# Reordering the start, the weight fetch and the seams of a two-layer attention kernel

## The chip, the cores and the metric

The kernel runs on one core of one Trainium2 chip. The metric is the device time of one execution in microseconds; the median of three runs is compared. The kernel before takes 3128.49 us (3128.35 to 3129.97).

## The reference, cut to what matters

The input x has two images of 256 channels on 64 x 64 places. Two layers run, each on a group-normalised x, each added to x.

```python
# layer 0: attention over all 4096 places, 8 heads of 32 channels
qkv = einsum('bchw,oc->bohw', gn(x), qkv_w) + qkv_b
out = softmax(q^T k / sqrt(32)) v            # per head, 4096 x 4096
x = x + out
# layer 1: two block attentions (64 places each) and a 3x3 convolution
q, k, v = 1x1 convolutions of gn(x); positions are added to q and k
ctx   = block attention over places of one phase, 1x1, bn_relu   -> feats
ctx2  = block attention inside 8x8 blocks (two 1x1 with bn_relu each for q and k), 1x1, bn_relu
f_all = fc_w mixes heads of q, k, v;  out_conv = 3x3 convolution of f_all
x = x + rate1 * ctx2 + rate2 * out_conv
```

## The kernel before, in words

The channels lie on 128 partitions in KC = 2 halves, the 4096 places in NT = 8 tiles of T = 512. The outer loop runs over the two images b; for each there are four stages, each with its own pools of PSUM banks.

**Start and projections** (b = 0). `load_x` (L66) loads eight tiles of x, 512 KB each, with one SyncE DMA per tile (L70). `group_stats` (L331) takes two bn_stats per tile on VectorE (L308), joins them (L312), averages over groups of eight channels by a small matmul (L315, L325), and `normalise` writes xn (L350). `fold_scores` (L186) prepares layer 1's score matrix from weights alone: the weights `w_by_out`, which eight DMAs on ScalarE's queue load at the head of the program (L85, 64 partitions each), `place_rows` and `grid` (L90, L92, SyncE). It transposes (L194), multiplies (L206: pt_meet and the two pt_g; L215: pt_key), copies out of PSUM on ScalarE (L195 to L224), and stores the result `kept_g` (L225). In the kernel before it stands ahead of the statistics in the program. `project0` (L392) computes keys and queries of four heads at a time (L400, evicted at L405 on ScalarE and L406 on VectorE, stored at L409), then values (L423), then the other four heads. Tiles for stores come from the pool w4, which has twelve buffers. The GpSimd queue loads the small constants and the projection weights (L104, L115, L126, L130), each an own DMA. The tile framework gives every DMA one of eight completion semaphores per kind of queue, in turn; a DMA whose semaphore is still in use by an earlier one waits for that one to land, and SyncE issues in order.

**Attention of layer 0.** `attention0` holds an order written out by hand for TensorE, ScalarE and VectorE. Scores go to three PSUM tiles of 3, 2 and 2 banks (sa, sb, sc, L498), ScalarE takes the exponential (L504), TensorE multiplies with the values (`quarters`, L514), and VectorE (L551) or accumulating DMAs (L561) add the rows of exponentials for the denominators. One step is a group g (half a head's queries) and a block j of 128 keys, NJ = 32 blocks. For the last group the sums of the last three blocks go through matmuls with ones (`sum_rows`, L575). `steps` (L714) issues them at block NJ - 2, ahead of that block's and the last block's av matmuls, into a bank of the tag sb. `finish_last` (L611) then copies the sums (L624), takes the reciprocal (L625), copies av (L627), multiplies, adds x and feeds the statistics of layer 1.

**First half of layer 1.** `layer1_first` (L1073) again writes out the order for TensorE, ScalarE and VectorE: it regroups x (`to_groups`, L1084 on ScalarE, L1087 on VectorE and GpSimd), finishes the statistics of the second channel half (`st.means`, `st.spread`, `st.variances`), and, for b = 0, multiplies weights together in between. That is the generator `fold_products`: each `next(fold)` runs it to its next yield; the five pieces are transposes of w3 (L245), its product (L251), transposes of fv, its product, and the small product pb_lr (L260 to L266). Then eight tiles of block attention follow, written to feats (L1068). From its end on VectorE also makes the 3x3 weights for b = 0 (`conv_weights`, L823 to L871), stored to `wf_kept` in DRAM (L865).

**Second half of layer 1.** `layer1_second` (L1209) writes the normalised image xp (`to_image`, L1218 to L1221, all on ScalarE), runs the second block attention for eight tiles (L1269, L1278, L993, L1011, L1057), and between them sixteen steps of the 3x3 convolution in a transformed form: GpSimd transforms the image (`conv_transform`, L916, L920), TensorE multiplies (L930), VectorE transforms back (L936 to L957). `fetch_conv_weights` (L877) loads all of the weights, 4 MB, with one SyncE DMA (L880); for b = 0 it also transposes them, 64 matmuls (L889), evicted by VectorE and ScalarE in turn (L892, L894), and stores them back (L895). TensorE's order is written out there; ScalarE's, VectorE's and GpSimd's are set by the framework's scheduler.

Of the kernel before, what the change touches and what calls it, by code (L numbers as in the profile page):

```python
# [9 lines left out]
F32 = mybir.dt.float32  # L10
I32 = mybir.dt.int32
F32R = mybir.dt.float32r
AF = mybir.ActivationFunctionType
# [4 lines left out]
P = 128  # L18
B, C, H, W = 2, 256, 64, 64
# [21 lines left out]
def direct_layers(ctx: ExitStack, tc: tile.TileContext, a: dict, out: bass.AP, bad: bass.AP):  # L41
# [24 lines left out]
    def load_x(b):  # L66
        tiles = []
        for t in range(NT):
            xt = xpool.tile([P, KC, T], F32, tag="x", name=f"x_{b}_{t}")
            nc.sync.dma_start(  # L70
                out=xt,
                in_=a["x"][b, :, t * T : (t + 1) * T].rearrange("(k p) n -> p k n", p=P),
            )
            tiles.append(xt)
        return tiles

    by_out = {}
    for name in ("w1", "w2"):  # L80
        by_out[name] = wpool.tile([P, KC, C], F32, tag="wp", name=f"{name}_by_out")

        for i in range(4):
            r = 64 * (i % 2)
            nc.scalar.dma_start(  # L85
                out=by_out[name][r : r + 64, i // 2, :],
                in_=a["wx"][int(name == "w2"), :, i, 0:P:4, :],
            )
# [3 lines left out]
    nc.sync.dma_start(out=grid, in_=a["loc"][1:3, 0:64])  # L92
    meet = const.tile([2, P], F32, name="meet")
    nc.vector.memset(meet, 0.0)
    x_first = load_x(0)

    ident = const.tile([P, P], F32, name="ident")
    make_identity(nc, ident)
# [250 lines left out]
    def normalise(dst, src, k, mean, rstd):  # L349
        return nc.vector.tensor_scalar(dst, src, mean[:, k : k + 1], rstd[:, k : k + 1], ALU.subtract, ALU.mult)  # L350
# [106 lines left out]
    def attention0(b, xts, held):  # L457
# [105 lines left out]
        def work_of(g, j):  # L563


            if (g, j) < (last, NJ - 2):
                add_rows(g, j)
            for part in (None,) if j in (0, NJ - 1) else range(2):
                if part == 1:
                    yield  # L570
                quarters(
                    sums[g], held["v"][:, (g // 2) % 2, j, :], lambda u: unit(g, j, u), j == 0, j == NJ - 1, part
                )
# [140 lines left out]
        def steps():  # L714

            for done in range(NH0 * 2 * NJ):
                g, j = divmod(done, NJ)
                if (g, j) == (last, NJ - 2):
                    assert len(places) == n_units
                    held["rows"] = psum["sc"].tile([P, 2, T], F32, tag="sb", name=f"rows_{b}")[:, 1, :]  # L720
                    for i in (NJ - 2, NJ - 1):
                        add_rows(g, i)
                    sum_rows(g, held["rows"])
                for _ in work_of(g, j):
                    yield done
                if g and j == 0:

                    for w in range(2):
                        dst = added[g - 1][w]
                        for s in range(2) if w == 0 else (slice(0, 2),):  # L730
                            nc.vector.tensor_add(dst[:, s, :], dst[:, s, :], acc[s] if w == 0 else pair)
                    waiting.clear()
                if g and j == 1:
                    wanted.append(late[0].send)
                if g and j in (9, 17):
                    next(late[0])
                for what in also.get((g, j), ()):
                    what()
                if j == 4 and g % 2 == 0 and g // 2 + 1 < NH0:
                    fetch_head(b, g // 2 + 1, held)  # L740
                if j == NJ - 1:
                    waiting.append(g)
                    avs = w4([P, 2, T], f"avs_{b}_{g}")
                    if g < last:
                        nc.scalar.copy(avs[:, 0, :], sums[g])
                    copied[g] = avs
                    late[:] = [finish(g)]
                    next(late[0])
                    if g + 2 < NH0 * 2:
                        fetch_queries(b, g + 2, held)  # L750
                yield done + 1
# [125 lines left out]
    def fetch_conv_weights(b):  # L877

        wf = vpool.tile([P, KC, UW, C], F32, tag="vw", name=f"wf_{b}")
        nc.sync.dma_start(out=wf, in_=wf_kept)  # L880
        if b > 0:
            return wf
        for pos in range(UW):
            r, q = divmod(pos, 4)
            pw = bank([P, KC, C], f"pw_{pos}")
            for k in range(KC):
                for m in range(2):
                    block = slice(m * P, (m + 1) * P)
                    nc.tensor.transpose(pw[:, k, block], wf[:, k, pos, block], ident)  # L889
            scale = (0.5 if r in (1, 2) else 1.0) * (0.5 if q in (1, 2) else 1.0)  # L890
            if pos % 2:
                nc.scalar.activation(wf[:, :, pos, :], pw, AF.Copy, scale=scale)  # L892
            else:
                nc.vector.tensor_scalar(wf[:, :, pos, :], pw, scale, None, ALU.mult)  # L894
        nc.sync.dma_start(out=wf_kept, in_=wf)  # L895
        return wf
# [176 lines left out]
    def layer1_first(b, xts, put, check, st):  # L1073
# [64 lines left out]
        with tc.manual_schedule(engines={E.PE, E.Activation, E.DVE}):  # L1138
            st.aggregate(second)
            fold = fold_products() if b == 0 else iter(())  # L1140
            put(nc.gpsimd.tensor_copy, (0, 1))
            for t in range(5, NT):
                to_groups(0, t, nc.gpsimd)
            pm, pv = bank([P, 1], f"pm_l1_{b}"), bank([P, 1], f"pv_l1_{b}")
            for t in range(3):
                to_groups(0, t, nc.scalar)
                next(fold, None)
            to_groups(0, 3, nc.scalar)
            if b:
                to_groups(0, 4, nc.scalar)  # L1150
            st.means(second, pm, nc.vector.tensor_copy)
            st.spread(second)
            firsts = [lambda t=t, m=m: project(t, m, slice(0, 1)) for t in range(2) for m in range(KC)]
            if b:
                firsts.pop(0)()
            next(fold, None)
            st.variances(second, pv)
            st.deviations(second, pv)
            shift_of(st, 1)
            if b == 0:  # L1160
                to_groups(0, 4, nc.scalar)
            put(nc.gpsimd.tensor_copy, (2, 3))
            n_act = 2 + b
            for t in range(NT):
                done = to_groups(1, t, nc.scalar if t < n_act else nc.vector)
            for _ in fold:
                pass
            check()
            for first in firsts:
                first()  # L1170
            for t in range(2):
                for m in range(KC):
                    project(t, m, slice(1, KC))
            at_grid(0)
# [34 lines left out]
    def layer1_second(b, xts, feats, mean, rstd, shift, pacc, following):  # L1209
# [5 lines left out]
            nc.gpsimd.memset(xp[:, k, PADW - 1, :], 0.0)  # L1215
            nc.gpsimd.memset(xp[:, k, 1 : PADW - 1, 0 : PADW : PADW - 1], 0.0)

        def to_image(t):  # L1218
            for k in range(KC):
                nc.scalar.activation(  # L1220
                    xp[:, k, 1 + 8 * t : 9 + 8 * t, 1 : 1 + W], xts[t][:, k, :].rearrange("p (r w) -> p r w", w=W),  # L1221
                    AF.Identity, bias=shift[:, k : k + 1], scale=rstd[:, k : k + 1],
                )

        results = {}
        turns = [divmod(n, 4) for n in range(4 * NT // 2)]
# [26 lines left out]

        if b:
            for t in range(3):
                to_image(t)
            ahead[0] = conv_transform(b, xp, *turns[0])
        pending = None
        for t in range(NT):
# [87 lines left out]
    for b in range(B):  # L1347
        xts = x_first if b == 0 else ahead["xts"]
        w0 = w0_first if b == 0 else ahead["w0"]
        with tc.tile_pool(name=f"ps0_{b}", bufs=8, space=PSUM) as psum["ps"]:  # L1350
            if b == 0:
                fold_scores()
            mean, rstd = group_stats(xts, "l0_0") if b == 0 else ahead["stats"]
            xn = apool.tile([P, KC, N], F32, tag="A", name=f"xn_{b}")
            for t in range(NT):
                for k in range(KC):
                    normalise(xn[:, k, t * T : (t + 1) * T], xts[t][:, k, :], k, mean, rstd)
            held = project0(b, xn, w0)
        if b == 0:
            load_layer1()  # L1360
        load_set(b, ("w3",) if b == 0 else ("g", "w3"))
        with tc.tile_pool(name=f"sc_{b}", bufs=1, space=PSUM) as psum["sc"]:
            put, check, st = attention0(b, xts, held)
        with tc.tile_pool(name=f"ps1_{b}", bufs=8, space=PSUM) as psum["ps"]:
            between = layer1_first(b, xts, put, check, st)
        with (
            tc.tile_pool(name=f"pacc_{b}", bufs=1, space=PSUM) as pacc,
            tc.tile_pool(name=f"ps2_{b}", bufs=4, space=PSUM) as psum["ps"],
        ):
            layer1_second(b, xts, *between, pacc, following)  # L1370
# [558 lines left out]
```

## Time and profile before

| | us |
|---|---|
| median of three runs | 3128.49 (3128.35 to 3129.97) |
| profiled execution | 3126.4 |
| its span, first to last instruction | 3124.2 |
| TensorE (PE) busy | 3030.2 |
| VectorE (DVE) busy | 2457.5 |
| ScalarE (ACT) busy | 2315.7 |
| GpSimd (POOL) busy | 843.4 |
| statistics of x wait for its loads, in total | 21.3 |
| first projection matmul starts | 37.18 |
| TensorE stands still before the transposes of the 3x3 weights | 10.18 |
| TensorE stands still before the mean of image 1's second statistics | 6.76 |

How to read it: PE is TensorE's matmuls, PEld its weight loads, which overlap them, SP is SyncE, whose queue issues most DMAs; a name with q is an engine's sequencer. A timeline line gives start, duration, engine, line, operation, output<-input, their shapes, the number of instructions merged, and in brackets the idle time before with what ended it. A line of waits gives the waiter, the releaser, total time, times and the longest wait. A line of windows gives a stretch, its length, each engine's busy time and instructions, TensorE's granted clock (1.00 is full), the mean busy share of the 16 DMA engines, and GB/s.

### The profile page before, as it was taken

The numbers are of one execution on the slowest core, as the hardware profiler recorded it, in microseconds if no ns is written. First come the engines' busy times: TensorE is split into PE (matmuls) and PEld (weight loads), VectorE is DVE, ScalarE is ACT, GpSimd is POOL, SyncE is SP. The second block draws the span as 40 slices with busy tenths as digits, with TensorE's granted clock in tenths as the row PEclk, the third lists the DMA queues.
The fourth block names the chain that finished last, engine by engine and source line by source line (L and its number), as shares of the span: only waits on it lengthen the run. The fifth ranks groups of instructions, "written<-read, shape, count | busy, mean of one in ns | idle before, by whom it ended". The sixth has DMA issues, their size and how long they took to land. (4 is left out here: it accounts for less than half of the span.)

```text
span 3124.2 us, 62490 instructions
## 1 busy us (share of the span) xinstructions
PE 3030.2 (97%) x25049; PEld 1826.3 (58%) x25049; DVE 2457.5 (79%) x3121; ACT 2315.7 (74%) x2440; POOL 843.4 (27%) x939
## 2 busy tenths in 40 slices
PE   6999999999999999989999999999999999899998
PEld 3555555555555556667765555555555555466765
DVE  4589988989899999846545999989999999834543
ACT  2599999999999984622236999999999999834333
POOL 3022222222223221055400222222222222305440
PEclk9999999999999999999999999999999999999999
DMA  7979678797887761221159686897878975700000
GB/s 231 260 145 184 136 157 168 154 183 143 171 175 157 146 133 35 75 110 54 38 185 259 134 176 145 163 172 147 169 164 166 180 159 117 179 4 4 21 14 22
DMA packets 241623, 424.37 MB, mean 136 GB/s; under 512 B 98744, under 2 KB 109548, under 8 KB 238892
## 3 DMA queue, kind: packets, MB, share of 16 engines
q0 software_dynamic: 95504, 238.36, 39.7%
q1 hardware_dynamic: 145292, 181.41, 21.6%
q8 instruction: 198, 3.24, 0.4%
q14 instruction: 101, 0.83, 0.1%
q10 hardware_dynamic: 528, 0.52, 0.1%
HBM read 119.03 MB, written 68.39 MB: 60 GB/s over the span
## 5 line engine op out<-in xcount | busy, mean ns | idle before, releaser
L551 DVE TENSOR_TENSOR e<-e,es 128x1024 f32<-128x1024 f32 (+1 forms) x956 | 1039.5, 1147 | 77.6 <-ACT es L504 76.3
L514 PE MATMUL av<-es,v 128*32 128x256 f32 (+1 forms) x9644 | 746.4, 390 | 0.0
L551 DVE TENSOR_TENSOR e<-e,v 128x1024 f32<-128x1024 f32 (+1 forms) x640 | 676.2, 1113 | 50.9 <-ACT v L504 49.7
L504 ACT ACTIVATE es<-sa 128x1536 f32<-128x1536 f32 (+1 forms) x444 | 635.9, 1432 | 94.4 <-PE sa L498 55.4
L498 PE MATMUL sa<-q,k 128*128 128x512 f32 x1736 | 560.7, 430 | 9.2 <-ACT avs L588 3.5
L514 PE MATMUL av<-v 128*32 128x256 f32 (+1 forms) x6228 | 506.5, 389 | 0.0
L514 PEld LDWEIGHTS av<-es,v 128*32 128x32 f32 x9644 | 316.0, 109 | 299.5 <-issue 161.0
L498 PEld LDWEIGHTS sa<-q,k 128*128 128x128 f32 x1736 | 279.9, 188 | 292.2 <-issue 135.0
L498 PE MATMUL sc<-q,k 128*128 128x512 f32 x1180 | 371.5, 396 | 3.3 <-ACT v L504 1.3
L498 PE MATMUL sb<-q,k 128*128 128x512 f32 x1180 | 370.7, 395 | 1.3 <-ACT v L504 1.3
L514 PEld LDWEIGHTS av<-v 128*32 128x32 f32 x6228 | 216.5, 109 | 178.5 <-issue 81.2
L504 ACT ACTIVATE es<-sc 128x1024 f32<-128x1024 f32 x296 | 307.2, 1038 | 0.0
L504 ACT ACTIVATE v<-sc 128x1024 f32<-128x1024 f32 x294 | 305.0, 1038 | 1.7 <-DMA acc<-v 1.7
L504 ACT ACTIVATE es<-sb 128x1024 f32<-128x1024 f32 x296 | 302.3, 1021 | 1.4 <-DMA acc<-es 1.2
L504 ACT ACTIVATE v<-sb 128x1024 f32<-128x1024 f32 x294 | 300.2, 1021 | 2.7 <-DMA acc<-v 2.7
L498 PEld LDWEIGHTS sc<-q,k 128*128 128x128 f32 x1180 | 209.8, 187 | 75.9 <-ACT es L504 12.3
L498 PEld LDWEIGHTS sb<-q,k 128*128 128x128 f32 x1180 | 220.8, 188 | 56.1 <-ACT v L504 2.2
L504 ACT ACTIVATE v<-sa 128x1536 f32<-128x1536 f32 (+1 forms) x146 | 209.3, 1433 | 34.8 <-PE sa L498 15.1
L930 PE MATMUL mm<-v,wf 128*128 128x256 f32 x1024 | 230.3, 383 | 4.3 <-DVE z L939 4.3
L561 POOL DMA_DIRECT2D es<-es x116 | 99.0, 853 | 465.7 <-ACT es L504 394.4
L930 PEld LDWEIGHTS mm<-v,wf 128*128 128x128 f32 x1024 | 195.2, 192 | 40.4 <-issue 12.6
L920 POOL TENSOR_TENSOR v<-col 128x512 f32<-128x512 f32 x128 | 165.0, 1314 | 195.2 <-DVE x L951 44.7
(261 smaller groups left out, 3171.9 us busy)
## 6 DMA issues: line engine op xcount, KB each, us to landing
acc<-es POOLq DMA_DIRECT2D x128, 512.0 KB, 6.4
acc<-v POOLq DMA_DIRECT2D x84, 512.0 KB, 6.4
es<-es POOLq DMA_DIRECT2D x136, 256.0 KB, 4.4
v<-es POOLq DMA_DIRECT2D x132, 256.0 KB, 5.0
k<-wk_halves SPq DMA_DIRECT2D x64, 512.0 KB
q<-wq_halves SPq DMA_DIRECT2D x256, 128.0 KB
v<-v POOLq DMA_DIRECT2D x90, 256.0 KB, 5.1
es<-v POOLq DMA_DIRECT2D x86, 256.0 KB, 4.1
```

What stands on the lines that cost most here:

```text
L498: nc.tensor.matmul(sc[:, i, :], held["k", g // 2][:, j * P : (j + 1) * P], held["q", g, u // 2][:, u % 2, :], start=True, stop=True,)
L504: nc.scalar.activation(dst, sc[:, i : i + m, :], AF.Exp, scale=SC0)
L514: nc.tensor.matmul(dst[HD0 * u : HD0 * u + HD0, n], lhs, rhs(u)[:, n], start=start, stop=stop)
L551: nc.vector.tensor_add(dst[:, s, :], dst[:, s, :], src)
L561: nc.gpsimd.dma_start(out=dst, in_=src, accum_op=ALU.add)
L920: (nc.gpsimd.tensor_add if plus else nc.gpsimd.tensor_sub)(dst, rows(one), rows(two))
L930: nc.tensor.matmul(mm[:, m, r, :], wf[:, k, 4 * r + q, m * P : (m + 1) * P], v[r // 2][:, r % 2, k, :], start=k == 0, stop=k == KC - 1,)
```

## The change

It has five parts.

1. x is loaded at the head of the program. The eight loads of `w_by_out` move from ScalarE's queue to SyncE's, behind x, and `fold_scores` is called behind `project0` instead of ahead of the statistics.
2. The 3x3 weights are fetched by four DMAs of four positions each (1 MB, runs of 4 KB) instead of one.
3. The row sums of the last group are issued at block NJ - 3, one block sooner, into a bank of the tag sa.
4. In `layer1_first` one more piece of `fold_products` runs ahead of the mean matmul.
5. In `layer1_second`, for b = 1, the first three tiles of the second channel half of xp are written by VectorE instead of ScalarE.

```diff
+    x_first = load_x(0)
...
-            nc.scalar.dma_start(
+            nc.sync.dma_start(
                 out=by_out[name][r : r + 64, i // 2, :],
...
-    x_first = load_x(0)
...
-            if (g, j) < (last, NJ - 2):
+            if (g, j) < (last, NJ - 3):
                 add_rows(g, j)
...
-                if (g, j) == (last, NJ - 2):
+                if (g, j) == (last, NJ - 3):
                     assert len(places) == n_units
-                    held["rows"] = psum["sc"].tile([P, 2, T], F32, tag="sb", name=f"rows_{b}")[:, 1, :]
-                    for i in (NJ - 2, NJ - 1):
+                    held["rows"] = psum["sc"].tile([P, 3, T], F32, tag="sa", name=f"rows_{b}")[:, 2, :]
+                    for i in (NJ - 3, NJ - 2, NJ - 1):
                         add_rows(g, i)
                     sum_rows(g, held["rows"])
...
-        nc.sync.dma_start(out=wf, in_=wf_kept)
+        for r in range(4):
+            nc.sync.dma_start(out=wf[:, :, 4 * r : 4 * r + 4, :], in_=wf_kept[:, :, 4 * r : 4 * r + 4, :])
...
             if b:
                 to_groups(0, 4, nc.scalar)
+            next(fold, None)
             st.means(second, pm, nc.vector.tensor_copy)
...
-        def to_image(t):
+        def to_image(t, both=False):
             for k in range(KC):
-                nc.scalar.activation(
-                    xp[:, k, 1 + 8 * t : 9 + 8 * t, 1 : 1 + W], xts[t][:, k, :].rearrange("p (r w) -> p r w", w=W),
-                    AF.Identity, bias=shift[:, k : k + 1], scale=rstd[:, k : k + 1],
-                )
+                dst = xp[:, k, 1 + 8 * t : 9 + 8 * t, 1 : 1 + W]
+                src = xts[t][:, k, :].rearrange("p (r w) -> p r w", w=W)
+                if both and k == 1:
+                    normalise(dst, src, k, mean, rstd)
+                else:
+                    nc.scalar.activation(
+                        dst, src, AF.Identity, bias=shift[:, k : k + 1], scale=rstd[:, k : k + 1]
+                    )
...
             for t in range(3):
-                to_image(t)
+                to_image(t, True)
...
-            if b == 0:
-                fold_scores()
             mean, rstd = group_stats(xts, "l0_0") if b == 0 else ahead["stats"]
...
             held = project0(b, xn, w0)
+            if b == 0:
+                fold_scores()
```

## The prediction

> **What bounds the kernel now.** I read the page's shares and slices first, then, gap by gap, the waits and the timeline where TensorE (PE) stands still.
>
> ```profile
> PE 3030.2 (97%) x25049; PEld 1826.3 (58%) x25049; DVE 2457.5 (79%) x3121; ACT 2315.7 (74%) x2440; POOL 843.4 (27%) x939
> ...
> PE   6999999999999999989999999999999999899998
> ```
>
> PE is busy 97% of 3124.2 us, so no edit can save more than the 94 us it stands still and what it runs at reduced clock. The first slice is the worst. There the statistics wait for x (VectorE's, DVE's, timeline), and the x loads wait on their own queue (the waits of SyncE, SP):
>
> ```profile
> SPq L70 <- DMA w_by_out<-in_wx_dram: 11.1, 4, 8.4
> ...
> 31.32 1.29 DVE L308 BATCH_NORM_STATS2 stats_l<-x 128x6 f32<-128x512 f32 x2 [0.33 <-DMA x<-in_x_dram]
> ...
> 37.18 15.62 PE L400 MATMUL p_wk<-xn,wqk 128*128 128x512 f32 x32 [1.13 <-DVE xn L350]
> ```
>
> Four x loads waited 11.1 us for completions of the weight loads of L85, so the last of eight tiles reaches DVE at 31.32 and the first projection starts at 37.18. The table by windows shows why those weights are slow (the last columns are PE's granted clock, DMA share, GB/s):
>
> ```profile
> 8.00:12.00 4.00, 0.00 (x0) 0.00 (x0) 1.29 (x2) 0.95 (x1) 3.45 (x8) 1.00 0.16 49
> 12.00:26.00 14.00, 2.15 (x8) 1.14 (x8) 2.57 (x4) 1.68 (x11) 10.18 (x19) 1.00 1.02 281
> 26.00:31.00 5.00, 2.91 (x11) 2.76 (x12) 3.86 (x6) 0.18 (x1) 4.65 (x20) 1.00 0.18 57
> ```
>
> A share of 0.16 is about two of sixteen DMA engines. From 37.18 to 121.63 PE has no gap; then it turns to attention:
>
> ```profile
> 123.19 0.97 PE L498 MATMUL sa<-q,k 128*128 128x512 f32 x3 [1.56 <-DVE hl_wq L406]
> ...
> 123.21 1.28 ACT L504 ACT_TABLE_LOAD   x1 [0.86 <-DVE hl_wq L406]
> ...
> 124.51 1.45 ACT L504 ACTIVATE es<-sa 128x1536 f32<-128x1536 f32 x1
> ```
>
> The next large gap is the fetch of the 3x3 weights (timeline, then windows):
>
> ```profile
> 1328.70 0.33 SPq L880 DMA_DIRECT2D wf<-wf_kept  x1
> ...
> 1341.27 8.68 PE L889 MATMUL pw<-ident,wf 128*128 128x128 f32 x64 [10.18 <-DMA wf<-wf_kept]
> ...
> 1331.10:1341.20 10.10, 0.00 (x0) 0.00 (x0) 0.00 (x0) 0.78 (x1) 9.87 (x8) 0.65 0.84 363
> 1341.27:1344.40 3.13, 3.13 (x15) 3.13 (x16) 0.99 (x2) 0.60 (x1) 3.05 (x3) 0.50 0.01 3
> 1344.40:1347.50 3.10, 3.10 (x31) 3.10 (x30) 2.35 (x4) 1.93 (x4) 0.35 (x1) 1.00 0.00 0
> ```
>
> PE waits 10.18 us for 4 MB and then runs 3.1 us at half clock (15 transposes against 31 in as long). The two seams of the second image:
>
> ```profile
> 2717.87 0.58 ACT L624 COPY kept<-rows 128x512 f32<-128x512 f32 x1 [3.02 <-PE rows L514]
> ...
> 2718.49 3.35 DVE L625 RECIPROCAL avs<-kept 128x512 f32<-128x512 f32 x1 [2.68 <-ACT kept L624]
> ...
> 2726.28 0.56 PE L315 MATMUL pm_l<-mv_l,group 128*128 128x1 f32 x2 [6.76 <-DVE mv_l L312]
> ...
> 2831.40 2.90 ACT L1220 ACTIVATE xp<-x,shift,rstd_l 128x512 f32<-128x512 f32 x4
> ...
> 2831.65 5.40 PE L1269 MATMUL phq_sr<-feats,wt_fq 128*128 128x512 f32 x8 [2.75 <-ACT feats L1068]
> ```
>
> The 6.76 us hang on a chain sums, copy, reciprocal, statistics. The 2.75 us hang on ScalarE (ACT), which places feats between image tiles.
>
> **What the Trainium skill says.** "DMA: Bandwidth & Descriptors", section "Why a DMA increments its semaphore by 16 and not by 1": the number of engines is the largest up to 16 that divides the slowest dimension of both sides. A load of L85 reads [2, 32, 256], so two engines; shares of 0.16 and 0.18 agree. The same page, "Issuing engines are not separate DMA queues": changing the issuing engine changes no bandwidth; the trace shows both queues sharing (share 1.02 at 12 to 26 us). "TensorE: Matmul & The Clock Gate", "Part 1: The HAM clock gate": about 3.4 us idle halves PE's clock, about 3.4 us of work restores it, and the window runs freely. The 0.50 after 10.18 and 6.76 us agrees; here 2.75 us also led to it.
>
> **The change part by part.** Sums are against the profiled execution: span 3124.2, its time 3126.4; the median 3128.5 is 2.1 above, and I carry differences to the median.
>
> *x first.* As the changed kernel's instructions stand, all eight x loads lead SP and wait for nothing; each L85 load waits for an x tile. x is 4.19 MB; at the 345 to 363 GB/s seen at 14 to 18 us that is 11.8 us, from about 2.4 us, so the last tile lands at 14.5. DVE takes 1.29 us per tile, as fast as they come: statistics end at 15.9. From their end to the first projection before was 37.18 - 32.6 = 4.6 us, of which 0.8 was the mean matmul standing behind the fold on PE: now 3.8, so 19.7. The projection weights come by GpSimd's (POOL's) queue, issued at 14.1 to 15.9, landing 7.4 us later under load; a bias load moves ahead of them (0.75). With x done by 14.5 I take 4 to 5 us: 19 to 20. I take 20.0 for the start, bounds 18.5 and 25. Gain 37.2 - 20.0 = 17.2. The half clock at the start (to 40.5 before, 3.3 us) stays. What x is moved past: L85's eight loads, two small loads and image 1's first x tile stand behind x on SP, ahead of the stores. On two engines L85 needs 256 KB each, some 12 us, so until about 27; the first store is due at 20 + 7.5 = 27.5. kept_at, in that queue, waits for at_query's loads (issued by 29.5, 4.1 to land), the sixth store is due at 33.7. I cost both at nothing: eight store buffers of 1.72 us cover it.
>
> *Fold behind the projections.* Its matmuls cost nothing while PE waited for x; now they stand between last projection and first score. ACT must evict the last projection (0.73 us), copy place and part (0.8), PE pt_meet (0.25), ACT meet (0.35), PE pt_key (0.4), then two products: 3.4 us each before at half clock, so 1.75 each: 6.0. ACT's copies 0.55, then three scores 1.0, then the table load 1.28, which in the changed order waits on PE as well: first exp at 8.9 us after the last projection, where it was 124.51 - 121.63 = 2.9. Cost 6.0, bounds 4.5 (table load not behind the scores) and 8. The fold's waits are at most 1.5 us, too short for the clock.
>
> *3x3 in four pieces.* Each piece has its own wait in PE's order. 4 MB took 12.45 us from issue to use, about 10 of transfer: pieces at 1332.4, 1334.9, 1337.4, 1339.9, if runs of 4 KB go as fast as 32 KB. Sixteen transposes take 1.75 us at full clock, so PE ends 1.8 after the last piece, 1341.7 instead of 1349.95: gain 8.2 (7 of wait, the rest clock). The first conv operand is ready at 1332.8, so nothing takes its place. Bounds: 6 (half clock stays) and 8.5; none if short runs were slow. In image 1 the load lies under 100 us of other work: nothing.
>
> *Last sums.* One block of eight av matmuls (0.9 us) moves behind the row sums; the last exp ends at 2713.24, before the sums reach its units. Image 1: gain 0.9, the clock loss stays. Image 0: the copy of av at 1168.0 doesn't move, the sums' copy does, so the statistics arrive 0.9 sooner, at 1173.3.
>
> *Seams.* In image 0 the second pm product goes ahead of the mean matmul. It waits for ACT's turned copies (1173.1 to 1173.7), so the mean runs at 1175.4 instead of 1174.3; pb_lr now fits under DVE's steps. Start of the projections 0.3 later: loss 0.3, bounds -1 and +1. In image 1 three xp tiles go to DVE, ahead of the bd copies on its queue: 3 x 0.54 = 1.6, bd 0.4 later, under ACT's slack (feats starts 0.8 after its product). But in ACT's changed order as many xp tiles stand ahead of the last feats as before, five, because later tiles move up. So 0, bounds -4.3 (2.2 us of ACT and half of the cold stretch) and +0.5.
>
> Sum: -17.2 + 6.0 - 8.2 - 0.9 + 0.3 = -20.0. Span 3104.2, profiled 3106.4, median 3108.5.
>
> **The rivals.** *Weights late:* the small POOL loads wait in turn for one another beside x, the projections start at 25: gain 12.2 - 6.0 + 8.2 + 0.6 = 15.0, 3113.5. For it: 7.4 us to land under load. Against: x is then done. *Handover shortened:* the xp tiles on DVE do close the 2.75 us and its cold stretch: 4.3 more, 3104.2. *Pieces no faster* (4 KB runs): 11.8, 3116.7. *Both short:* start at 27, no gain from pieces: 4.8, 3123.7, no difference that can be measured. *Slower:* SP's queue holds the stores behind L85 and kept_at; after eight buffers, 13.8 us, PE stops. That decides from a hold of 20 us past that, first store after 62 us; at 70 us 3137. Against: L85 is done by 27.
>
> **How the numbers follow.** Forecast 0.60, weights late 0.17, handover 0.12, pieces 0.05, both short 0.03, slower 0.03. A measurement here tells 0.2%, 6.3 us, from no change. Faster 0.94, same 0.03, slower 0.03. Range 3101 to 3117: it holds the first four cases; their spread beyond it and the last two are left out. Window phases of the clock add some 2 us either way.
>
> **What would show it.** First projection at 20 (25 or later: weights late). First exp 8.9 after the last projection. First transpose some 1.5 us after its predecessor with no half clock. Mean matmul of image 1 after 5.9 us. The wait for feats still 2.75. A gap inside the projections, or one over 10 us at the fold, makes the prediction wrong.

## The result and the profile after

Timed side by side, the changed kernel takes 3120.55 us (median of 6, 3116.14 to 3121.84) and the kernel before 3130.18 us (6, 3128.35 to 3132.29): ratio 0.9967 (95% interval 0.9954 to 0.9980), faster by 9.6 us. Half of the 20 us that the prediction summed up are there; 3120.55 lies above its range. Measured again later, the ratio was 0.9956 (0.9943 to 0.9970).

From the page of the kernel after, TensorE's (PE's) busy time and its forty slices:

```profile
PE 3034.8 (97%) x25049; PEld 1830.3 (59%) x25049; DVE 2459.9 (79%) x3124; ACT 2314.6 (74%) x2437; POOL 844.6 (27%) x939
...
PE   7999999999999999999999999999999999899998
```

The same 25049 matmuls are busy for 4.6 us longer than before, with 4.1 us less span: PE waits less, and more of its work runs at half clock.

One profile a side misleads here. The first profiled execution of the kernel before (3126.4 us, span 3124.2) was faster than each of its timed runs, of which the lowest is 3126.84; two more profiles have spans of 3131.0 and 3130.4. The kernel after has 3120.1 and 3117.5. So stages are compared over three profiles of before and two of after, by marks that both traces have (us; "61st exponential" is that of L504 in image 0, "turn" the last exponential of image 0, "mean matmul" the second of the two at L315):

| stage | before (3) | after (2) | change | predicted |
|---|---|---|---|---|
| start to first projection | 37.18, 37.57, 37.48 | 21.99, 21.67 | -15.6 | -17.2 |
| projections | 84.45, 84.57, 85.25 | 84.79, 85.46 | +0.4 | 0 |
| last projection to 61st exponential | 72.70, 72.94, 73.05 | 81.61, 79.86 | +7.8 | +6.0 |
| attention of image 0 | 965.85, 966.01, 965.88 | 963.63, 964.58 | -1.8 | 0 |
| turn to second block attention | 121.17, 121.15, 122.82 | 123.97, 122.42 | +1.5 | +0.3 |
| from there to the last 3x3 transpose | 68.60, 70.74, 70.41 | 64.00, 63.91 | -6.0 | -8.2 |
| to the last exponential of image 1 | 1362.26, 1364.75, 1363.37 | 1364.64, 1364.62 | +1.2 | 0 |
| to the mean matmul of image 1 | 14.28, 14.31, 14.30 | 14.29, 14.30 | 0.0 | -0.9 |
| to the second block attention | 105.16, 105.18, 105.18 | 105.21, 105.23 | 0.0 | 0 |
| to PE's end | 283.82, 284.88, 283.82 | 284.81, 284.83 | +0.6 | 0 |
| PE's end to the span's end | 8.74, 8.89, 8.85 | 11.14, 10.65 | +2.1 | 0 |

The changes sum to -9.7, close to the timed 9.6. Now the lines that answer to those of before. The start, in the timeline after:

```profile
14.86 1.29 DVE L308 BATCH_NORM_STATS2 stats_l<-x 128x6 f32<-128x512 f32 x2 [0.19 <-DMA x<-in_x_dram]
15.31 1.78 POOL L126 DMA_DIRECT2D wqk<-in_wk_dram  x2
...
21.99 2.04 PE L400 MATMUL p_wk<-xn,wqk 128*128 128x512 f32 x2 [3.27 <-DMA wqk<-in_wk_dram]
```

x is complete as predicted (last statistics 14.86 to 16.15). The bracket of the last line is new: PE waits for the key weights, which land 6.5 us after their issue; the matmul starts 6.7 us after it.

The turn to attention, timeline and table by windows (stretch, length, busy time of PE, PEld, DVE, ACT, POOL, then PE's granted clock, DMA share, GB/s):

```profile
108.78 0.24 PE L206 MATMUL pt_meet<-query_part,place 128*2 128x3 f32 x4 [1.80 <-ACT query_part L202]
...
109.78 1.13 PE L206 MATMUL pt_g<-w_by_out 128*128 128x256 f32 x4
...
111.78 2.05 PE L206 MATMUL pt_g<-w_by_out 128*128 128x256 f32 x4
...
115.86 1.65 PE L498 MATMUL sa<-q,k 128*128 128x512 f32 x3 [0.53 <-ACT w_at L224]
...
118.87 1.45 ACT L504 ACTIVATE es<-sa 128x1536 f32<-128x1536 f32 x1
```

```profile
106.00:111.00 5.00, 2.80 (x17) 1.74 (x16) 1.41 (x2) 2.41 (x11) 0.00 (x0) 1.00 1.05 401
111.00:115.00 4.00, 4.00 (x19) 3.64 (x18) 0.00 (x0) 0.44 (x2) 0.00 (x0) 0.54 0.98 374
115.00:118.00 3.00, 2.47 (x7) 2.00 (x8) 0.00 (x0) 0.87 (x3) 0.00 (x0) 0.50 0.47 117
118.00:122.00 4.00, 2.84 (x7) 1.73 (x7) 0.00 (x0) 3.99 (x4) 0.00 (x0) 0.50 0.97 266
```

No wait exceeds 1.80 us, yet after five microseconds with 2.80 busy the clock falls to a half and stays there for 13.65 us (6.83 in the second profile). The four matmuls of the second product's first step take 2.05 us, those of the first product 1.13; together the two products at the end of the fold take 5.55 us (109.78 to 115.33) where 3.5 were predicted, the first three scores 1.65 instead of 0.97. The first exponential comes 12.1 us after the last projection (11.5 in the second profile), not 8.9.

The fetch of the 3x3 weights:

```profile
1323.34 4.02 SPq L881 DMA_DIRECT2D wf<-wf_kept  x4
...
1330.29 7.20 PE L890 MATMUL pw<-ident,wf 128*128 128x128 f32 x48 [4.57 <-DMA wf<-wf_kept]
...
1338.04 1.94 PE L890 MATMUL pw<-ident,wf 128*128 128x128 f32 x16 [0.56 <-DMA wf<-wf_kept]
```

PE's wait fell from 10.18 to 4.57 us, not to 1.5: the first piece can be used 6.95 us after its issue, the last 14.7 us after it, where the single load took 12.6. In the second profile PE waits 2.93 us, the first piece is used after 5.32 us, and the transposes still end at the same time (16.6 us after the issue in both).

The second statistics of image 1:

```profile
2709.42 0.59 ACT L624 COPY kept<-rows 128x512 f32<-128x512 f32 x1 [2.16 <-PE rows L514]
2710.04 3.35 DVE L625 RECIPROCAL avs<-kept 128x512 f32<-128x512 f32 x1 [1.82 <-ACT kept L624]
...
2711.22 7.68 POOL L1088 TENSOR_SCALAR xg<-x,mean_l,rstd_l 128x512 f32<-128x512 f32 x3 [9.90 <-PE av L514]
...
2713.62 0.58 ACT L627 COPY avs<-av 128x512 f32<-128x512 f32 x1
...
2714.23 1.35 DVE L628 TENSOR_TENSOR avs<-avs 128x512 f32<-128x512 f32 x1 [0.84 <-ACT avs L627]
...
2718.70 0.56 PE L315 MATMUL pm_l<-mv_l,group 128*128 128x1 f32 x2 [6.77 <-DVE mv_l L312]
```

The wait is 6.77 us as before. Counted from the last exponential (2712.21 before, 2704.62 after) the sums' copy starts 0.86 us sooner, the mean matmul 0.01 us later. The multiply, VectorE's L628, had to wait another 0.84 us for its second input, ScalarE's copy of av.

### The profile page after: what moved, and what is told of

Its sections match the earlier page's. It is cut to its first block, busy times and chain, and to the rows that moved or that the text cites. A ratio compares the mean times of both kernels' runs of the same rounds, so it can differ in the third digit from the quotient of the medians.

```text
span 3120.1 us, 62504 instructions
## 1 busy us (share of the span) xinstructions
PE 3034.8 (97%) x25049; PEld 1830.3 (59%) x25049; DVE 2459.9 (79%) x3124; ACT 2314.6 (74%) x2437; POOL 844.6 (27%) x939
## 5 line engine op out<-in xcount | busy, mean ns | idle before, releaser
L504 ACT ACTIVATE es<-sa 128x1536 f32<-128x1536 f32 (+1 forms) x444 | 636.0, 1432 | 94.6 <-PE sa L498 56.1
L504 ACT ACTIVATE es<-sc 128x1024 f32<-128x1024 f32 x296 | 306.5, 1036 | 0.0
L504 ACT ACTIVATE v<-sc 128x1024 f32<-128x1024 f32 x294 | 304.4, 1035 | 1.0 <-PE sa L498 0.9
L504 ACT ACTIVATE es<-sb 128x1024 f32<-128x1024 f32 x296 | 302.0, 1020 | 1.3 <-DMA acc<-es 1.3
L504 ACT ACTIVATE v<-sb 128x1024 f32<-128x1024 f32 x294 | 300.0, 1020 | 2.8 <-DMA acc<-v 2.8
L504 ACT ACTIVATE v<-sa 128x1536 f32<-128x1536 f32 (+1 forms) x146 | 209.3, 1434 | 35.6 <-PE sa L498 16.5
```

Of the source, the lines that this page charges most:

```text
L504: nc.scalar.activation(dst, sc[:, i : i + m, :], AF.Exp, scale=SC0)
```

## The experiments

All are edits of the changed kernel where nothing else is said. A time is a median beside runs of the kernel before, and a gain in us is the ratio's, which can differ from that of the two medians; "one run" is a single time, read for its stages only.

**One part alone.** The kernel before with part 1.

> The kernel before with part 1 alone (x first, fold behind the projections). Theory A (each part of the change fell short in its own stage): first projection at 22.0 with a wait for the projection weights, first exponential about 11.9 us after the last projection, so 5 to 6 us ahead of before at the second attention block; total 5 to 7 us under before. Theory B (part 1 brings the predicted 11.2 us and the shortfall is drift in attention): some 11 us under before.

Measured: 3120.7 against 3133.82 us, ratio 0.9969 (0.9958 to 0.9980). First projection 21.99; first exponential 11.6 us after the last projection; 61st exponential 5.9 us ahead of the first profile of before. The stages are those of theory A; the timed gain, 9.7 us by the ratio (6 to 13; the medians are 13.1 apart), holds both theories' sums.

The kernel before with part 2.

> The kernel before with part 2 alone (3x3 weights in four pieces). Theory A: first piece usable 7 us after its issue, last one 14.7 us after it (12.6 in one piece), transposes end 4.6 to 5.0 us sooner than before; total about 5 us under before. Theory B (pieces work as predicted, 8.2 us, and the rest was lost elsewhere): 8 us under before and no half clock at the transposes.

Measured: 3125.03 us, ratio 0.9975 (0.9969 to 0.9982), by which it is 7.8 us less. First piece used 7.4 us after its issue, last 15.1; stage 64.38 us, against 68.60 to 70.74. Against the first profile of before that is a gain of 4.2, too small for the timed one; against all three it is 5.5, just below the timed interval (5.6 to 9.7). The stage is that of theory A.

The kernel before with parts 1 and 2.

> The kernel before with parts 1 and 2 alone. Theory A (parts 3 to 5 bring nothing and lengthen the last stage): from the second seam's first phase matmul to the end 291 to 292.5 us as before, against 295 to 296 in the changed kernel; total some 2 to 4 us under the changed kernel. Theory B (the long last stage is chance or belongs to parts 1 and 2): 295 us here too.

Measured: 3121.51 us, ratio 0.9964 (0.9950 to 0.9979). From image 1's second block attention PE needs 282.1 us to its end, the changed kernel 284.8, but the end came 10.09 us after that, not 8.3 to 8.9 as in before and with one part: 292.2 in all. Theory A by its number, though the total isn't told from the changed kernel's.

**What holds the start.** First the key weights' loads were to go ahead of the bias loads:

```diff
+    load_heads(wqk_first[:, 0], "wk0")
     vecs = load_const("vecs", [P, NVEC], a["vecs"])
```

> The changed kernel with the two loads of the key weights issued on the GpSimd queue ahead of the small loads. Theory A (the 3.3 us wait of the first projection is for the issue of these loads, late behind the bias loads that wait in turn): first projection at 19.0 to 19.5, 2.5 to 3 us under the changed kernel. Theory B (any transfer beside x is slow, and these delay x): start stays at 21 or later, no gain.

Measured: 3120.3 us, 0.9965 (0.9954 to 0.9977); first projection 22.77. But the loads were still issued at 15.52, behind the biases: the edit didn't do what it says, and the run is a repetition of the changed kernel. Then on ScalarE's queue (`nc.scalar.dma_start` for wk0):

> The changed kernel with the two loads of the key weights on ScalarE's queue, which is empty at the start (the run before meant to move them on GpSimd's queue, where the framework's scheduler put them back behind the bias loads). Theory A (they are issued too late): first projection at 19.0 to 20.0, 2 to 3 us sooner than in the changed kernel. Theory B (a load beside x is slow wherever it is issued): still 21.5 or later.

One run, first projection 27.28. The first of the two loads was issued at 17.27: SyncE's and ScalarE's queues draw on the same eight completion semaphores, and the one that it was given was held by the second load of w_by_out, issued at 6.04 and landed at 17.25. ScalarE's part of the statistics stood behind. The number is theory B's, but the loads were late again, so the run tells the theories apart no more than the one before. Then with the weights' tile allocated ahead of place_rows:

```diff
     x_first = load_x(0)
+    wqk_first = w4([P, 2, KC, NH0 * HD0], "wqk0_0")
+    load_heads(wqk_first[:, 0], "wk0")
     by_out = {}
```

> The changed kernel with the tile of the key and query weights allocated, and the key weights' two loads written, ahead of everything but x (two runs before left these loads late: the pool gives tiles in program order, and place_rows, the tile ahead, sits behind x on SyncE's queue; on ScalarE's queue they waited for x's own semaphores). Theory A (issue time is what made them late): issued at 1 to 3, first projection at 19.8 to 20.5, without a wait for them. Theory B (what runs beside x is slow however early): 21.5 or later.

One run. Now they are early, in this timeline:

```profile
1.30 2.05 POOL L84 DMA_DIRECT2D wqk<-in_wk_dram  x2 [0.85 <-POOLq L1931]
...
15.77 2.58 DVE L315 BATCH_NORM_STATS2 stats_l<-x 128x6 f32<-128x512 f32 x4 [0.31 <-DMA x<-in_x_dram]
...
22.05 2.08 PE L407 MATMUL p_wk<-xn,wqk 128*128 128x512 f32 x2 [1.14 <-DVE xn L357]
```

PE no longer waits for the weights, and starts no sooner: x ends at 18.35 instead of 16.15. That is theory B's number, but not its reason: the weights were there in time, and the time moved from one load to the other. What else runs beside them are the w_by_out loads. Those put behind the first store of the queries, each cut in two:

```diff
+                if b == 0 and nm == "wq0" and g == 0 and t == 0:
+                    with tc.issue_after(stored.ins):
+                        load_by_out()
...
-                out=by_out[name][r : r + 64, i // 2, :],
+                        out=by_out[name][r + 32 * j : r + 32 * j + 32, i // 2, :],
```

> The changed kernel with the loads of w_by_out moved behind the first store of the queries, in sixteen loads of 32 rows. Theory A (the start is bound by what the DMA engines must carry ahead of it, and these loads, on two engines, run among x and the key weights): key weights land within 4 us of their issue, first projection at 19.8 to 20.8. Theory B (the key weights' own short runs and x alone bound the start): still 21.5 to 22.5.

One run. The weights are issued at 13.85, nothing waits for them, and the start is 20.23:

```profile
13.85 1.85 POOL L129 DMA_DIRECT2D wqk<-in_wk_dram  x2
...
14.90 1.29 DVE L311 BATCH_NORM_STATS2 stats_l<-x 128x6 f32<-128x512 f32 x2 [0.30 <-DMA x<-in_x_dram]
...
20.23 4.63 PE L403 MATMUL p_wk<-xn,wqk 128*128 128x512 f32 x5 [1.48 <-DVE xn L353]
```

Theory A holds: the weights land 3.1 us after their issue instead of 6.5, and are issued 1.5 us sooner than in the first profile of the changed kernel, while x ends at 16.19, as in the changed kernel (16.15). From there VectorE's chain (xn) is the last to arrive. So w_by_out beside the key weights cost 1.4 to 1.8 us of the start.

**What the fold costs.** Cut into five steps by `yield`, each run behind a tile of the second key projections:

```diff
                     in_=pair.bitcast(F32),
                 )
+                if g:
+                    next(fold, None)
```

> The changed kernel with the fold cut into five steps that run between the key projections of the second four heads. Theory A (the fold cost 9 us because of the waits of its chain, the table load behind it and the clock it lost): first exponential 2.9 us after the last projection, the fold's matmuls cost 3 to 4 us of TensorE time in the projections, no half clock at the start of attention; 4 to 5 us under the changed kernel. Theory B (its small matmuls themselves cost the time and the clock): projections 7 us or more longer, half clock among them, no gain.

Measured: 3119.03 us, 0.9960 (0.9947 to 0.9973), which can't be told from the changed kernel. Projections 89.67 us (85.1 in the changed kernel), no half clock in them, first exponential 3.5 us after. From the first projection to the 61st exponential it takes 161.7 us instead of 165.3 to 166.4, against 157.2 in the first profile of before. So 3.6 to 4.7 us of the fold's cost were waits and clock, and 4.5 us stay. One point of theory A failed: 3.4 us at half clock still came, from 115.42 on, just ahead of the first exponential. As one block with its waits, called ahead of `heads4("wk0", 1)`:

> The changed kernel with the fold as one block, its waits kept, ahead of the key projections of the second four heads instead of behind the last projection. Theory A (the fold's own short waits and small matmuls read as idle to the clock): a stretch at half clock begins within some 5 us of the fold, among the projections, and the projections grow by 8 us or more. Theory B (the clock falls only because the first scores and the table load follow the fold): no half clock there, projections grow by 6 to 7 us, first exponential 3 us after the last projection.

One run, 3119.9. The longest wait in the fold, which begins at 79.1, and the windows around it:

```profile
80.22 0.24 PE L206 MATMUL pt_meet<-query_part,place 128*2 128x3 f32 x4 [0.85 <-ACT query_part L202]
...
80.00:83.50 3.50, 2.88 (x20) 2.57 (x21) 0.00 (x0) 1.01 (x9) 0.00 (x0) 1.00 0.97 290
83.50:87.00 3.50, 3.50 (x13) 2.79 (x12) 0.00 (x0) 0.56 (x4) 0.00 (x0) 0.50 0.99 130
87.00:90.30 3.30, 3.30 (x5) 1.28 (x4) 0.00 (x0) 0.57 (x1) 0.00 (x0) 0.50 0.89 153
```

Waits here are at most 0.85 us, and the clock falls 4.4 us after the fold's start; the 512-column matmuls behind it then run at half clock without a gap. Projections 93.63 us, 8.5 more. Theory A: the fold itself costs the clock. Whether its short waits do it or its narrow matmuls isn't separated.

**The pieces.** Two of eight positions (`range(2)`, `8 * r : 8 * r + 8`):

> The changed kernel with the 3x3 weights in two pieces of eight positions (runs of 8 KB) instead of four. Theory A (each load has a fixed time of some 4 us from issue to first use beside its bytes, and 4 KB runs carry about a tenth less): first piece used 9 us after its issue, second 13.5 us after it; transposes end within 1 us of the four pieces. Theory B (the runs of 4 KB are what costs): second piece 12.6 us after the issue and the end 1.5 us or more sooner than with four.

One run. First piece used 7.75 us after its issue, transposes end 17.3 us after it (15.8 to 17.2 in the profiles with four pieces), stage 66.40, of which 1.8 us are a later issue. The transposes run without a gap from the first piece on, with a half-clock stretch of 6.8 us that begins 2.0 us ahead of them, so the second piece held nothing. The end is as theory A said, its 9 us for the first piece is not, and theory B's gain didn't come. What the packets of the trace do tell is the transfer: from the first packet to the last the 4 MB took 10.8 us here, 10.9 to 11.0 as one load, and 11.9 to 13.2 in four pieces. So theory B has the transfer right. Whether the 4 KB runs or the number of loads slow the four isn't separated.

**The sums.** Without ScalarE's copy of av:

```diff
-            nc.scalar.copy(y, sums[g])
-            nc.vector.tensor_mul(y, y, avs[:, 1, :])
+            nc.vector.tensor_mul(y, sums[g], avs[:, 1, :])
```

> The changed kernel with ScalarE's copy of av out of PSUM left out: VectorE multiplies straight from PSUM, the result is the same. Theory A (part 3 gained nothing because this copy, behind two image tiles on ScalarE, became the last to arrive): from the last exponential to the mean matmul of image 1 13.4 to 13.6 us instead of 14.3. Theory B (the sums were never the last): 14.3 as before.

One run, 14.30 us, the number of theory B. These are VectorE's lines, and GpSimd's beside them:

```profile
2711.91 7.67 POOL L1087 TENSOR_SCALAR xg<-x,mean_l,rstd_l 128x512 f32<-128x512 f32 x3 [9.55 <-PE av L514]
...
2714.18 0.69 DVE L627 TENSOR_TENSOR avs<-av,avs 128x512 f32<-128x512 f32 x1
2714.90 1.37 DVE L628 SCALAR_TENSOR_TENSOR avs<-avs,bv_last,x_last 128x512 f32<-128x512 f32 x1
...
2717.03 1.79 DVE L632 COPY stats_l<-some 32x6 f32<-32x6 f32 x4
```

The multiply came 8.90 us after the last exponential instead of 9.61 and took 0.69 us instead of 1.35, so the copy of av had held it. But the add behind it took 1.37 instead of 0.75, and the small copies 1.79 instead of 1.01, which used up the gain. (In image 0 the same edit put the mean 1.3 us later.) GpSimd's tiles ran beside all of them. These tiles put behind GpSimd's first copies of the result as well:

```diff
-            put(nc.gpsimd.tensor_copy, (0, 1))
-            for t in range(5, NT):
-                to_groups(0, t, nc.gpsimd)
+            with tc.issue_after(put(nc.gpsimd.tensor_copy, (0, 1))):
+                for t in range(5, NT):
+                    to_groups(0, t, nc.gpsimd)
```

> The changed kernel with VectorE multiplying av straight from PSUM, and GpSimd's three image tiles of the seam issued behind its first copies of the attention's result, so that they don't run beside VectorE's multiply and add. Theory A (VectorE's operations with two operands in SBUF wait for GpSimd, and this took the gain of the earlier sums): multiply and add take 0.7 and 0.75 us, and from the last exponential to the mean matmul of image 1 12.7 to 13.5 us instead of 14.3. Theory B (something else holds the statistics): 14.3.

One run, 3130.19, some 10 us more than the changed kernel:

```profile
2717.27 0.69 DVE L627 TENSOR_TENSOR avs<-av,avs 128x512 f32<-128x512 f32 x1
2718.00 0.75 DVE L628 SCALAR_TENSOR_TENSOR avs<-avs,bv_last,x_last 128x512 f32<-128x512 f32 x1
...
2720.20 7.64 POOL L1088 TENSOR_SCALAR xg<-x,mean_l,rstd_l 128x512 f32<-128x512 f32 x3
...
2727.89 2.08 PE L1108 MATMUL py<-xg,wt_g 128*128 128x512 f32 x2 [5.32 <-POOL xg L1088]
```

Multiply and add take what theory A said, and the mean comes after 13.84 us, between the two theories; the small copies again ran beside GpSimd's tiles and took 1.95 us. The last line shows what stood behind: PE's first projection of the stage reads every tile of xg, GpSimd's too. In the changed kernel these end at 2718.90, 0.2 us ahead of that projection (2719.12). So even with VectorE free, part 3 could have brought that projection only 0.2 us. These tiles wait for the av matmuls and start 6.60 us after the last exponential in either kernel, so part 3 didn't move them. With the edit that projection came 5.0 us later in image 1 and 2.8 us later in image 0.

**Part 5 undone.**

> The changed kernel with part 5 undone (all tiles of xp on ScalarE). Theory A (part 5 costs a gap of 0.75 us at the first 3x3 step of image 1 and gains nothing): from the second seam's first phase matmul to TensorE's end some 0.8 us less than in the changed kernel, with the same wait for feats of 2.75. Theory B (part 5 is neutral): no difference beyond a half-clock stretch.

One run: PE's last stage 282.12 us, the wait for feats 2.75. Without part 5 the stage takes 282.1 us (four profiles without half clock in it), 283.5 to 283.8 (four with 3.4 us of it) or 284.9 (one with 6.8); with part 5 283.2 (one without), 284.5 to 284.8 (nine with 3.4) or 285.8 (one with 6.8). So part 5 costs 1.0 us, theory A, and 3.4 us of half clock 1.2 to 1.7. In the changed kernel three quarters of the 1.0 us are this wait, which all eleven profiles with part 5 have (0.72 to 0.87 us) and none without:

```profile
2863.07 3.26 PE L931 MATMUL mm<-v,wf 128*128 128x256 f32 x14 [0.75 <-DVE z L940]
```

**Versions.** Spread fold, key weights first, multiply from PSUM, GpSimd behind, no part 5:

> Changed kernel without part 5, with the key weights' loads first, the fold spread over the projections, the multiply from PSUM and GpSimd's tiles behind. Theory A (these are the terms that fell short, 2, 4, 1 and 0.8 us): first projection at 20.2, 60th exponential at 182 (188.4 in the changed kernel), 7 to 8 us under the changed kernel, ratio to before 0.994 to 0.995. Theory B (drift in attention outweighs them): no better than the changed kernel, 0.9965.

3122.54 us, 0.9964 (0.9952 to 0.9976): theory B by the number, but not by drift. The version carries what GpSimd's tiles cost in pool_behind, 5.0 us in image 1 and some 3 in image 0, and its first projection is at 22.08, not 20.2, as in wk_first. Spread fold, late w_by_out, no part 5:

> The changed kernel with the fold spread over the projections, the loads of w_by_out late as in the run above, and part 5 undone. Theory A: first projection at 20.5, 60th exponential at 182 to 183 (188.4 in the changed kernel), last stage 1 us shorter; 6 to 8 us under the changed kernel, ratio to before 0.994 to 0.995. Theory B: drift outweighs it, the same as the changed kernel.

3113.93 us (5 runs), 0.9949 (0.9935 to 0.9962). First projection 20.64 and PE's last stage 283.78 are as expected. The 61st exponential at 184.96 is 2 to 3 us late: from the first projection to it 164.3 us pass, so here the spread fold brought only 1 to 2 us, and why isn't known. Beside it the changed kernel:

> The changed kernel itself, once more, on the same chip as the runs above. Theory A: each of its stages as in its first profile within 1 us (first projection 22 to 23, 60th exponential less the last projection 79 to 82, pieces 16.5 us from issue to the last transpose), attention of either image within 3 us of it, ratio to before 0.996 to 0.998. Theory B (its first profile was an unlucky one): 0.994 or less.

3119.31 us (5 runs), 0.9956 (0.9943 to 0.9970). The stages are those of theory A but for the first projection, 21.67, a little sooner; the ratio lies just under its range. The two kernels are 5.4 us apart by medians, with overlapping intervals; 3 to 4.5 us of the difference of their profiles lie in stages that the edits touch. Likely better, not shown.

**The kernel before, twice more.**

> The kernel before itself, profiled again: its first profile (3126.4) is faster than all 43 of its timed runs of the studies so far but one. Theory A (stages of attention and half-clock stretches drift by a few us in every kernel): first projection at 37.2 and fold, pieces and seams as in the first profile within 1 us, the difference of some 4 to 6 us in the long attention stages. Theory B (the fetch of the 3x3 weights varies, which would explain that four pieces gained 7.8 us by the clock and 4.2 by the stage): issue to last transpose 24 us or more instead of 21.2.

> The kernel before a third time, for the spread of each stage. Theory A and B as for the run ahead of it.

3133.14 and 3132.5. Stages as in the table: some 2 us of the difference to the first profile lie in the 3x3 stage, where VectorE had the last weights ready 1.4 to 1.7 us later and more transposes ran at half clock; the fetch itself took 12.4 and 12.3 us (12.6). In the attention of image 0 there is no difference (965.85 to 966.01), in the stretch to the end of image 1's attention 1.1 to 2.5 us; the rest are half-clock stretches in the seams and the last stage. So the drift of theory A is there, but little of it where A put it, and B's 24 us did not come.

## Why the prediction was wrong, step by step

**x first, -17.2, measured -15.6.** x, statistics and chain came as worked out. The failed term is "With x done by 14.5 I take 4 to 5 us" for the key weights: 6.7 us, and 3.1 to land once w_by_out was out of the way (by_late). The term left out that w_by_out, which the same paragraph moves behind x, is still under way then. Rival "weights late" had the late weights, at 22 instead of 25, though not w_by_out as the cause. Stores behind w_by_out cost nothing, as said.

**Fold behind, +6.0, measured +7.8.** The failed step is "The fold's waits are at most 1.5 us, too short for the clock". "TensorE: Matmul & The Clock Gate", section "Part 1: The HAM clock gate", speaks of an idle window of about 3.4 us; the measurement decides, and here a chain of matmuls of 2 to 256 columns with waits of 1.80 us at most did it (0.85 in fold_mid). All twelve profiles with the fold behind the projections lost the clock there, none of the four with it ahead of the statistics. The size follows: with 3.4 us of half clock the stage took 78.9 us, which is before plus the predicted 6.0; with 6.8 us 79.8; with 10 to 14 us 81.2 to 83.1.

**Four pieces, -8.2, measured -6.0.** The failed step is "pieces at 1332.4, 1334.9, 1337.4, 1339.9": it put the last piece 11.2 us after its issue, less than the 12.6 of the single load (12.45 in its sum). Measured 14.7, and for the first 7.0 and 5.3 where 3.7 was said. The sum took 10 us of transfer and 1.2 us for the rest. By the packets, first to last, the transfer took 11.0 us as one load and 12.8 and 12.5 in pieces, which its "if runs of 4 KB go as fast as 32 KB" left open. The rest is 1.36 us from the issue to the first packet and 0.5 us from the last packet to PE's start. "DMA: Bandwidth & Descriptors", section "Anatomy of one DMA — SWDGE (gpsimd) path", gives some 2 us fixed per transfer, most of it the receipt; that is for another issuing path, and here the total of 1.9 us is near it, but most of it lies at the start. The half clock, said to go, stayed: it covers 3.1 to 5.1 us of the transposes in the three profiles of before, 3.0 and 6.8 us after. Where the load is issued at the same point of the stage (47.3 us into it, first profile of before) the gain is 4.6 us; the mean is 6.0 because VectorE was later in two profiles.

**Last sums, -0.9, measured 0.0.** The copy did come 0.86 us sooner. The failed step is that the statistics follow it: I followed one chain only. The multiply also needs ScalarE's copy of av, behind two image tiles, and that came 0.84 us after the reciprocal. Behind it stand GpSimd's tiles. "SBUF — State Buffer", section "SBUF: two separate sides", says that a VectorE operation with two inputs in SBUF and a GpSimd operation that reads SBUF shut each other out; psum_mul and pool_behind agree: the multiply took 0.69 us with one input in PSUM and 1.35 with both in SBUF, the add 0.75 us without GpSimd's tiles and 1.37 beside them, though behind a held multiply it took its 0.75 beside them too. They don't agree that the second waits for the whole of the other's instruction: the multiply of the changed kernel (2714.23 to 2715.59) begins and ends inside one GpSimd tile (2713.80 to 2716.35, though spans on GpSimd are rough). And GpSimd's tiles end within 0.2 us of the projection that reads them.

**Seams.** Image 0 was costed at +0.3: the projections began 18.26 us after the last exponential, 18.22 before, so the order cost nothing. The mean came 1.0 us later, as worked out. The stage grew by 1.5 us where a half-clock stretch fell on it. Such stretches come with before's order too (projections 18.2 to 19.8 us after; stage 121.2 to 122.8 without part 4, and 121.2 to 124.0 in the eleven profiles with it whose sums and GpSimd tiles are the changed kernel's); I count them as drift, not to part 4. Image 1: the wait for feats stayed (2.79), as said; missed was a 3x3 step that then waited for VectorE, which part 5 gave three tiles more (0.75 us), 1.0 us with what follows.

**What no step had.** The end after PE's last matmul, +2.1 us. The output leaves 1.6 us after PE's end in either kernel. In the trace after, one more 8 KB packet of the instruction queue lands 0.14 us before the program ends; before, the packet like it comes after the end. Fourteen profiles of programs with parts 1 and 2 show 9.8 to 11.1 us, the fifteenth (two_pieces, with fewer loads) 8.9, before and the single parts 8.3 to 8.9. Whether the program's length sets it is not shown; the cause stays open.

Shortfall: start 1.6, fold 1.8, pieces 2.2, end 2.1, seam of image 0 1.2, sums 0.9, last stage 0.6; projections and attention add up to 0.2 the other way: 10.2 of the 20. The range was too narrow because the sum let the clock depend on each wait's length alone, took a transfer's time from larger ones, and had no term for the end.

## What to carry to other kernels

A chain of small matmuls that hid behind a wait costs more than its own time once it stands on the path: here a half-clock stretch came with it each time. Cut up and laid between large matmuls it took 1 to 5 us less in three profiles (fold_spread, best1, best2), though no total shows it alone. A transfer cut into pieces lets the first user start sooner, but the last piece came later (14.7 us instead of 12.6 in four pieces of 4 KB runs), and the gain is less than the wait it shortens. Before taking an engine's wait as gain, list the second and third input of the instruction that ends it, with the time each arrives.

## What the runs showed that I had not expected

PE's clock fell after waits of 0.85 us at most (fold_mid). A load issued 14 us earlier started nothing sooner, since x beside it then ended 2.2 us later (wk_first). The span of the kernel before differs by 6.8 us between profiles (3124.2 and 3131.0), with half-clock stretches that, but for the one that the end cuts off, come in multiples of 3.41 us.
